# Nine steps of an attention period laid out anew: the seven products in the first five, another order of query and key tiles

## The chip, the cores and the metric

The kernel runs on one core of a Trainium2 chip. The metric is device time in microseconds (us) of one execution. All arithmetic shown is float32, except the small bfloat16 helpers named below.

## The reference, cut to what matters

```python
x = L0_attn_x                                      # (8, 1024, 512)
x = _layernorm(x + attention(x, W_Q, W_K, W_V, W_O))
x = _layernorm(x + moe(x, router_w, router_b, expert_w, expert_b))
# attention: 16 heads of 32, causal
Q, K, V = x @ W_Q.T, x @ W_K.T, x @ W_V.T
probs = softmax(where(causal, Q K^T / sqrt(32), -inf))
y = (probs V) @ W_O.T
# moe: 8 experts, the one with the largest router probability, times that probability
```

The softmax needs the sum of each row, and the kernel also takes each row's extreme first.

## The kernel before

**Periods and steps.** There are B = 8 batches and NG = 4 groups of HG = 4 heads, so NP = 32 periods `n`, each for one batch `b` and one head group `g = n % 4`. A period has NU = 9 steps `u`. One step does, for three different periods at once:

1. the exact scores and their exponentials of period n (`exps`, L806): a bfloat16 matmul that puts in the row constants (L820), four heads' matmuls K·Q on top (L826), two ScalarE exponentials from PSUM to `p` (L832, the first head alone, then the other three), and on the diagonal blocks GpSimd's `affine_select` (L836). `s_units` says which key tile `j` and query half `c` a step takes: one pair, or two pairs that share 512 columns.
2. the row extremes of a later unit, LEAD = 12 units ahead (`maxima`, L697): four heads' matmuls (L709) into four tiles of the pool `ps_m`, then for each head a VectorE pass that writes the raw scores to SBUF and takes the row minimum of the negated scores (L719). `m_units` says which query tile `qt` and which columns a unit takes: query tile 7 first, 3 last. Some units hold two parts, so their VectorE passes are twice as many and half as long. The raw rows live in NRAW = 7 buffers; ScalarE later takes exp with the row's own constant and sums it (`exp_sums`, L744, its instruction L762), as many rows in a step as a credit allows, or as the next unit's need of buffers forces. After the last row of a period ScalarE takes Ln (L750, with two table loads), VectorE splits the result in three bfloat16 parts (`split_maxima`), and `turn_maxima` in the last step transposes them (L783) and copies them to `mT` (L787).
3. a fill of 16 or 32 TensorE instructions: either a product of the queries' and keys' projection two periods ahead, or a whole projection (V, or the output projection, or in batch 0 the router's preparation).
4. the values matmul of the step (`values`, L850, L863) and its addition into `ctx` (copy L882 where it is the first, add L886 otherwise).

**The seven products.** The projection to Q and K of a period is made as a two by two block product with seven instead of eight products (`class seven`). Each product is eight matmul pairs (L629), each of seven is evacuated by VectorE into one or two places of Q and K (L642 add, L646 copy). GpSimd makes their operands, sums of blocks of x and of weights (L606): `begin` (three sums, first and second operand), `second`, `third`, `fourth`, each queued at the end of a step. Before, the products lie in steps 0 (two), 1, 2 (two), 3 and 5; a "short" step is one with one product, `HALVES_AT = (1, 3, 5)`. Whole projections lie in `WHOLE_AT = (4, 6, 7, 8)`. In a short step the fourth head's minimum is put behind the product's evacuation.

**Order.** The program is written out by hand under a manual schedule, each engine's queue in the order of the calls. In a step VectorE has: minima of three or four heads, a `normalize` of finished output rows if the step is "quiet" (L942), the fill's evacuation, the deferred head, small matmuls' evacuation, the `ctx` addition, then statistics of output rows. The PSUM is divided as `ps_m` (four banks in rotation: four heads' maxima, the second product of a step, small matmuls, values), `ps_f` (one bank, shared by the first head's scores and the fill) and `ps_s` (three banks, the other heads' scores). Small matmuls are the router's logits (L990, 8 or 16 instructions as rows of the trace count them) and the turn of logits (L1009). Batch b+1's x is loaded in period g = 1 (`load_x`, SP queue) into the buffers that batch b used. `pieces` are parts of the routing of tokens, which start after period 26 and are put into quiet steps. Before the first period there are LEAD lead steps with maxima and a fill only; after the last period comes the experts' part, one tile after the other.

```python
for u in range(NU):
    t = n * NU + u + LEAD
    exps(n, u)
    ...
    left = maxima_at(t, HG - 1 if short else HG)
```

Of the kernel before, what the change touches and what calls it, by code (L numbers as in the profile page):

```python
# [26 lines left out]
def attn_moe_kernel(ctx: ExitStack, tc: tile.TileContext, x, xT, wqT, wkT, wvT, woT, rwT, rb, ewT, eb, out):  # L27
# [446 lines left out]
    def attention():  # L474
# [10 lines left out]
        with ExitStack() as st:  # L485
# [72 lines left out]
            def run(made, name):  # L558
                out, rest = made(bank(name, ps_f))
                out()  # L560
                if rest:
                    rest()
# [24 lines left out]
            class seven:  # L587
# [45 lines left out]
                def steps(self):  # L633
# [11 lines left out]
                    def copy(dst):  # L645
# [3 lines left out]
                        0: [self.product(self.s, self.t[0], copy(k[1])), self.product(a11, b11, copy(q[0]))],  # L649
                        1: [self.product(self.s, self.t[1], add((q[1], q[0])))],  # L650
                        2: [
                            self.product(a12, b21, add((q[0], q[0]))),
                            self.product(a22, self.t[0], add((q[1], q[1]), op=ALU.subtract)),
                        ],
                        3: [self.product(self.s, b22, add((k[0], k[1])))],
                        5: [self.product(self.s, self.t[1], add((q[1], q[1]), (k[1], k[1])))],
                    }, {0: self.second, 1: self.third, 3: self.fourth}
# [29 lines left out]
            m_units = [[part(7, 0, 512)], [part(7, 512, 1024)]]  # L687
            m_units += [[part(6, 0, 512)], [part(6, 512, 896), part(0, 0, 128, 384, 896)]]
            m_units += [[part(5, 0, 512)], [part(5, 512, 768), part(1, 0, 256, 256, 768)]]
            m_units += [[part(4, 0, 512)], [part(4, 512, 640), part(2, 0, 384, 128, 640)]]  # L690
            m_units += [[part(3, 0, 512)]]
# [42 lines left out]
            HALVES_AT = (1, 3, 5)  # L734
            WHOLE_AT = (4, 6, 7, 8)
# [56 lines left out]
            s_units = [((0, 0),), ((0, 1), (0, 3)), ((0, 2), (1, 6)), ((1, 0),), ((1, 5), (1, 7)), ((1, 1),), ((1, 4),)]  # L792
            s_units += [((1, j),) for j in range(2, 4)]
# [3 lines left out]
            def blocks(u):  # L797

                at = 0
                for c, j in s_units[u]:  # L800
                    q0 = max(c * 512, j * P)
                    w = c * 512 + 512 - q0
                    yield c, j, q0, w, at
                    at += w

            def exps(n, u):  # L806
# [10 lines left out]
                for c, j, q0, w, at in blocks(u):  # L817
# [15 lines left out]
                for c, j, q0, w, at in blocks(u):  # L833
# [16 lines left out]
            def values(n, u, pool=ps_m):  # L850
# [5 lines left out]
                for c, j, q0, w, at in blocks(u):  # L856
# [4 lines left out]
                    for h in range(HG):  # L861
# [4 lines left out]
                            start=new, stop=(c, j) == [x for x in s_units[u] if x[0] == c][-1],  # L866
                        )
                    if g == NG - 1 and c == NC - 1:
                        v_free.append(v_slot.pop((b, j)))
# [156 lines left out]
            LEAD = NU + 3  # L1026
# [26 lines left out]
            for c in range(NC):  # L1053
                for name in ("wq", "wk"):
                    run(project_qk(0, c, name), f"{name}_0_{c}")
# [19 lines left out]
            for n in range(NP):  # L1075
# [21 lines left out]
                late = HALVES_AT[1]  # L1097
                if g == 0:
                    if b:
                        small_ones[late].append(lambda ps: logits_part(b - 1, [NG - 1], False, ps))  # L1100
                    small_ones[HALVES_AT[2]].append(lambda ps: logits_part(b, [0, 1], True, ps))
                elif g == 1:
                    if b:
                        small_ones[HALVES_AT[2]].append(lambda ps: turn_logits(b - 1, ps))
                    small_ones[late].append(lambda ps: logits_part(b, [2, 3], True, ps))
# [7 lines left out]
                for u in range(NU):  # L1113
# [3 lines left out]

                    quiet = u not in behind and (u != HALVES_AT[-1] or n + 3 >= NP)

# [34 lines left out]
                    if g == 1 and b + 1 < B and u == late:  # L1154
                        for c in range(NC):
                            load_x(b + 1, c)
# [74 lines left out]
```

## Time and profile before

| what | value |
|---|---|
| times of three runs | 2178.26, 2180.58, 2180.76 us (median 2180.58) |
| the profiled execution | 2186.84 us, span 2184.9 us |
| granted TensorE clock, mean | 0.993 |
| TensorE matmul busy | 2110.7 us (97%) |
| VectorE, ScalarE, GpSimd busy | 1629.0 (75%), 1547.2 (71%), 784.6 (36%) us |
| before the first scores | 0 to 82.73 us |
| periods 0 to 25 | 82.7 to 1536.9 us |
| the experts' part | about 1880 to 2184.9 us |

Period 11 (head group 3) starts at 692.87 us; the lengths of its nine steps, from first score matmul to first score matmul, are 6.48, 5.18, 6.50, 5.20, 6.81, 5.41, 6.71, 6.50 and 7.17 us, in all 55.96 us. Periods 8, 9, 10 and 11 (head groups 0 to 3) start at 523.75, 580.05, 636.53 and 692.87 us, period 12 at 748.83 us.

Line numbers are those of the kernel before. An instruction group is named by line, engine, operation, and out<-in with the program's tile names. A bracket "[0.59 <-DVE big L642]" says that the engine sat idle so long before the instruction and what ended it. A TensorE row counts an instruction's records, two for one float32 matmul here, and overlaps with its neighbours; its busy time includes time in which a started group waits.

### The profile page before, as it was taken

The page shows a single profiled execution, that of the slowest core. Times are in us where ns is not written, and L with a number is a line of the kernel's source. Part 1 is how long each engine was busy: PE and PEld are TensorE (multiplying, and loading weights), DVE is VectorE, ACT ScalarE, POOL GpSimd, SP SyncE. Part 2 cuts the span into 40 slices and gives each one's busy share as a digit, 9 for nine tenths or more (in the row PEclk, how much of TensorE's full clock was granted, in tenths as well). Part 3 has the DMA queues.
Part 4 walks back from the last instruction along what each step waited for, and adds up shares of the span by engine and source line. Part 5 has one row for each costly group of instructions (what it writes and reads, how often), then busy time and mean ns, then how long its engine had stood idle before and what let it go on. Part 6 is the DMA issues. An engine that isn't in the chain of part 4 may idle for free. (4 is left out here: it accounts for less than half of the span.)

```text
span 2184.9 us, 52442 instructions
## 1 busy us (share of the span) xinstructions
PE 2110.7 (97%) x20251; PEld 829.7 (38%) x20251; DVE 1629.0 (75%) x4960; ACT 1547.2 (71%) x2979; POOL 784.6 (36%) x757
## 2 busy tenths in 40 slices
PE   8989999999999999999999999999999888999998
PEld 2333333333333333333333333333333333344443
DVE  4777777877787778777877787778778885478776
ACT  3688877788777777777777787777777576243443
POOL 3233333333333333333333333333333243255554
PEclk9999999999999999999999999999999999999999
DMA  3001000110021002100210020001001032443432
GB/s 117 1 18 48 1 2 11 69 40 1 7 73 40 2 2 73 45 2 2 74 45 2 2 73 16 31 1 65 20 11 45 7 126 74 135 150 126 135 125 83
DMA packets 46743, 103.79 MB, mean 48 GB/s; under 512 B 5982, under 2 KB 8030, under 8 KB 46368
## 3 DMA queue, kind: packets, MB, share of 16 engines
q1 hardware_dynamic: 34464, 65.02, 8.6%
q0 software_dynamic: 11360, 35.40, 5.1%
q8 instruction: 161, 2.64, 0.5%
q14 instruction: 86, 0.70, 0.1%
q10 hardware_dynamic: 672, 0.02, 0.0%
HBM read 66.87 MB, written 35.39 MB: 47 GB/s over the span
## 5 line engine op out<-in xcount | busy, mean ns | idle before, releaser
L832 ACT ACTIVATE p<-s 128x512 f32<-128x512 f32 x584 | 559.0, 1010 | 396.0 <-PE s L826 395.9
L762 ACT ACTIVATE raw<-raw,low 128x1024 f32<-128x1024 f32 (+7 forms) x1024 | 779.1, 770 | 44.4 <-DVE low L719 44.4
L719 DVE CUSTOM_DVE_ANT_0 raw<-m,wide_mask 128x512 f32<-128x512 f32 (+3 forms) x1024 | 571.5, 587 | 148.9 <-PE m L709 148.9
L836 POOL TENSOR_SCALAR_AFFINE_SELECT p<-p 128x512 f32<-128x512 f32 x256 | 158.8, 639 | 810.5 <-ACT p L832 810.5
L719 DVE CUSTOM_DVE_ANT_0 raw<-m,wide_mask,lowA 128x256 f32<-128x256 f32 (+3 forms) x512 | 273.3, 548 | 140.3 <-PE m L709 140.3
L863 PE MATMUL pv<-p,V 128*32 128x512 f32 (+3 forms) x3072 | 307.6, 493 | 21.0 <-DVE lowA L719 7.1
L709 PE MATMUL m<-big 32*128 32x512 f32 (+3 forms) x3072 | 316.4, 488 | 0.0
L826 PE MATMUL s<-big 32*128 32x512 f32 (+3 forms) x3072 | 313.8, 491 | 0.0
L606 POOL TENSOR_TENSOR xs<-big 128x1024 f32<-128x1024 f32 x60 | 142.4, 2373 | 351.6 <-PE f L629 351.6
L437 PE MATMUL y<-big,gT 128*128 x568 | 255.8, 594 | 2.6 <-ACT gT L429 2.6
L674 PE MATMUL f<-big 128*32 128x512 f32 x2048 | 233.0, 595 | 0.0
L926 PE MATMUL f<-wo,ctx 128*32 128x512 f32 x1920 | 218.4, 595 | 0.8 <-ACT p L832 0.8
L709 PEld LDWEIGHTS m<-big 32*128 32x128 f32 x3072 | 175.2, 186 | 87.7 <-issue 64.3
L762 ACT ACTIVATION_READ_ACCUMULATOR raw<-raw,low 128x1 f32 x1024 | 199.7, 195 | 0.0
L629 PE MATMUL f<-xs,ws 128*32 128x512 f32 x1440 | 173.2, 598 | 1.1 <-ACT p L832 0.9
L886 DVE TENSOR_TENSOR ctx<-pv,ctx 128x384 f32<-128x384 f32 (+2 forms) x250 | 146.7, 587 | 32.8 <-PE pv L863 31.0
L863 PEld LDWEIGHTS pv<-p,V 128*32 128x32 f32 x3072 | 90.6, 110 | 201.4 <-issue 95.1
L820 PE MATMUL s<-mT,ones_b 3*128 3x512 bf16 (+3 forms) x1536 | 132.5, 331 | 23.0 <-DVE big L642 8.9
L826 PEld LDWEIGHTS s<-big 32*128 32x128 f32 x3072 | 142.8, 188 | 21.2 <-issue 15.9
L437 PEld LDWEIGHTS y<-big,gT 128*128 128x128 f32 x568 | 102.6, 191 | 105.7 <-issue 101.7
L455 ACT ACTIVATE yrstd<-ymv,eps 128x1 f32<-128x1 f32 x71 | 20.9, 295 | 151.5 <-DVE ymv L453 146.5
L464 POOL DMA_INDIRECT out<-g,r_sca x71 | 83.2, 1172 | 123.4 <-ACT g L463 90.1
(229 smaller groups left out, 2253.7 us busy)
## 6 DMA issues: line engine op xcount, KB each, us to landing
h<-in_x SPq DMA_DIRECT2D x64, 256.0 KB, 3.8
x<-h SPq DMA_DIRECT2D x64, 256.0 KB, 2.0
big<-in_xT SPq DMA_DIRECT2D x15, 1024.0 KB, 7.3
big<-in_ewT SPq DMA_DIRECT2D x8, 1024.0 KB, 8.0
bias<-in_eb SPq DMA_DIRECT2D x1, 2048.0 KB, 12.0
g<-x,r_gat POOLq DMA_INDIRECT x71, 3.5
out<-g,r_sca POOLq DMA_INDIRECT x71, 2.9
big<-in_xT SPq DMA_DIRECT2D x4, 256.0 KB, 5.7
```

The source lines that it names most:

```text
L437: nc.tensor.matmul(y_ps, lhsT=gT[:, k, :], rhs=big[:, bass.ds(e, 1), k, :].rearrange("p a o -> p (a o)"), start=(k == 0), stop=(k == NK - 1),)
L629: nc.tensor.matmul(ps, lhsT=w[:, k][:, m], rhs=x[:, k, :], start=start, stop=stop)
L674: lambda ps, k, m, start, stop: nc.tensor.matmul(ps, lhsT=xT_sb[b, c][:, k, o : o + P][:, m], rhs=w_sb["wv"][:, k, :], start=start, stop=stop,
L709: nc.tensor.matmul(tiles[h][:, at : at + c1 - c0], lhsT=Q[n][r, qt * P : (qt + 1) * P], rhs=K[n][r, c0:c1], start=True, stop=True,)
L719: nc.vector.tensor_tensor_reduce(out=raws[n, h][:, to : to + w], in0=tiles[h][:, at : at + w], in1=wide_mask[:, 640 - w :] if last else wi ...
L762: nc.scalar.activation(a[:, to : to + w], a[:, to : to + w], AF.Exp, scale=-1.0, bias=low[n][:, qt, h : h + 1], accum_out=sums[n][:, qt, h ...
L826: nc.tensor.matmul(tiles[h][:, at : at + w], lhsT=K[n][r, j * P : (j + 1) * P], rhs=Q[n][r, q0 : q0 + w], start=False, stop=True,)
L832: nc.scalar.activation(p[:, hs], scores, AF.Exp, scale=-1.0)
L836: nc.gpsimd.affine_select(out=p[:, :, at : at + P], in_=p[:, :, at : at + P], compare_op=ALU.is_ge, fill=0.0, base=0, pattern=[[0, HG], [1 ...
L863: nc.tensor.matmul(ps[h * HD : h * HD + HD, parts[c][1] - w : parts[c][1]], lhsT=V[b, j][:, ch : ch + HD], rhs=p[:, h, at : at + w], start ...
L886: nc.vector.tensor_tensor(to, here[:, new:], to, ALU.add)
L926: lambda ps, k, m, start, stop: nc.tensor.matmul(ps, lhsT=ctx_of(b * NG + k, qt * P, P)[:, m], rhs=w_sb["wo"][:, k, :], start=start, stop= ...
```

## The change

It moves work among the nine steps and alters three orders:

- the products: step 0 one, step 1 two, step 2 one, step 3 two, step 4 one; the product with two places of evacuation is the second of step 3. Short steps become 0, 2 and 4, whole projections 5 to 8; `fourth` is queued after step 2, `begin` after step 4.
- `m_units` begins with query tile 4 and ends with 7 (tile 3 just before it); `LEAD` is NU + 4 = 13 instead of 12.
- `s_units` begins with (1,0), (0,0); the last period keeps the old order as `s_last`. Buffers of V are freed at a key tile's last use (`last_use`).
- small matmuls go to steps 5 and 6 (in group 1 also to step 1) instead of 3 and 5; quiet steps become 4 to 8 (5 to 8 in group 1); the two halves of the next x are loaded after steps 3 and 4.
- the first four projections use the four banks of `ps_m` in place of the one of `ps_f`.

```diff
-            def run(made, name):
-                out, rest = made(bank(name, ps_f))
+            def run(made, name, pool=ps_f):
+                out, rest = made(bank(name, pool))
...
-                        0: [self.product(self.s, self.t[0], copy(k[1])), self.product(a11, b11, copy(q[0]))],
-                        1: [self.product(self.s, self.t[1], add((q[1], q[0])))],
-                        2: [
-                            self.product(a12, b21, add((q[0], q[0]))),
+                        0: [self.product(self.s, self.t[0], copy(k[1]))],
+                        1: [self.product(a11, b11, copy(q[0])), self.product(self.s, self.t[1], add((q[1], q[0])))],
+                        2: [self.product(self.s, b22, add((k[0], k[1])))],
+                        3: [
                             self.product(a22, self.t[0], add((q[1], q[1]), op=ALU.subtract)),
+                            self.product(self.s, self.t[1], add((q[1], q[1]), (k[1], k[1]))),
                         ],
-                        3: [self.product(self.s, b22, add((k[0], k[1])))],
-                        5: [self.product(self.s, self.t[1], add((q[1], q[1]), (k[1], k[1])))],
-                    }, {0: self.second, 1: self.third, 3: self.fourth}
+                        4: [self.product(a12, b21, add((q[0], q[0])))],
+                    }, {0: self.second, 1: self.third, 2: self.fourth}
...
-            m_units = [[part(7, 0, 512)], [part(7, 512, 1024)]]
+            m_units = [[part(4, 0, 512)], [part(4, 512, 640), part(2, 0, 384, 128, 640)]]
+            m_units += [[part(5, 0, 512)], [part(5, 512, 768), part(1, 0, 256, 256, 768)]]
             m_units += [[part(6, 0, 512)], [part(6, 512, 896), part(0, 0, 128, 384, 896)]]
-            m_units += [[part(5, 0, 512)], [part(5, 512, 768), part(1, 0, 256, 256, 768)]]
-            m_units += [[part(4, 0, 512)], [part(4, 512, 640), part(2, 0, 384, 128, 640)]]
-            m_units += [[part(3, 0, 512)]]
+            m_units += [[part(3, 0, 512)], [part(7, 0, 512)], [part(7, 512, 1024)]]
...
-            HALVES_AT = (1, 3, 5)
-            WHOLE_AT = (4, 6, 7, 8)
+            HALVES_AT = (0, 2, 4)
+            WHOLE_AT = (5, 6, 7, 8)
...
-            s_units = [((0, 0),), ((0, 1), (0, 3)), ((0, 2), (1, 6)), ((1, 0),), ((1, 5), (1, 7)), ((1, 1),), ((1, 4),)]
-            s_units += [((1, j),) for j in range(2, 4)]
+            s_units = [((1, 0),), ((0, 0),), ((1, 1),), ((0, 2), (1, 6)), ((1, 2),), ((1, 5), (1, 7)), ((1, 4),)]
+            s_units += [((0, 1), (0, 3)), ((1, 3),)]
+
+            s_last = [s_units[i] for i in (1, 7, 3, 0, 5, 2, 6, 4, 8)]
+            last_use = {j: u for u, unit in enumerate(s_units) for _, j in unit}
...
-                    if g == NG - 1 and c == NC - 1:
+                    if g == NG - 1 and last_use[j] == u:
                         v_free.append(v_slot.pop((b, j)))
...
-            LEAD = NU + 3
+            LEAD = NU + 4
...
-                    run(project_qk(0, c, name), f"{name}_0_{c}")
+                    run(project_qk(0, c, name), f"{name}_0_{c}", ps_m)
...
-                late = HALVES_AT[1]
+                late = WHOLE_AT[0]
                 if g == 0:
+                    small_ones[late].append(lambda ps: logits_part(b, [0, 1], True, ps))
                     if b:
-                        small_ones[late].append(lambda ps: logits_part(b - 1, [NG - 1], False, ps))
-                    small_ones[HALVES_AT[2]].append(lambda ps: logits_part(b, [0, 1], True, ps))
+                        small_ones[late + 1].append(lambda ps: logits_part(b - 1, [NG - 1], False, ps))
                 elif g == 1:
+                    small_ones[1].append(lambda ps: logits_part(b, [2, 3], True, ps))
                     if b:
-                        small_ones[HALVES_AT[2]].append(lambda ps: turn_logits(b - 1, ps))
-                    small_ones[late].append(lambda ps: logits_part(b, [2, 3], True, ps))
+                        small_ones[late].append(lambda ps: turn_logits(b - 1, ps))
...
-                    quiet = u not in behind and (u != HALVES_AT[-1] or n + 3 >= NP)
+                    quiet = u not in behind and (n + 3 >= NP or u not in ((3, 4) if g == 1 else (3,)))
...
-                    if g == 1 and b + 1 < B and u == late:
-                        for c in range(NC):
-                            load_x(b + 1, c)
+                    if g == 1 and b + 1 < B and u in (3, 4):
+                        load_x(b + 1, 4 - u)
```

## The prediction

> Times in a step count from its first score matmul (L820); s, m, f, pv are the TensorE parts scores (L820/L826), maxima (L709), fill, values (L863). A period n is nine steps u.
>
> **What bounds it now.** First the page: TensorE leads.
>
> ```profile
> span 2184.9 us, 52442 instructions
> ...
> PE 2110.7 (97%) x20251; PEld 829.7 (38%) x20251; DVE 1629.0 (75%) x4960; ACT 1547.2 (71%) x2979; POOL 784.6 (36%) x757
> ```
>
> Then the table of windows, cut at the steps of period 11: its length is 55.96 us, and the neighbours of the same head group differ by 0.01. So one period, counted well, is the kernel. Columns: window, length, busy time and count of each engine.
>
> ```profile
> 711.03:716.23 5.20, 5.20 (x56) 1.83 (x52) 3.74 (x11) 4.35 (x10) 1.04 (x1) 1.00 0.00 0
> 716.23:723.04 6.81, 6.81 (x92) 2.94 (x89) 4.96 (x22) 5.37 (x12) 2.56 (x3) 1.00 0.02 4
> 723.04:728.45 5.41, 4.83 (x48) 1.58 (x44) 3.73 (x10) 4.27 (x11) 1.26 (x1) 1.00 0.00 0
> 728.45:735.16 6.71, 6.70 (x60) 2.23 (x61) 4.38 (x12) 4.60 (x10) 3.15 (x4) 1.00 0.01 2
> sum 55.96, PE 55.28 PEld 20.84 DVE 40.25 ACT 44.63 POOL 18.39; mean PE 6.14 PEld 2.32 DVE 4.47 ACT 4.96 POOL 2.04
> ```
>
> TensorE idles 0.68 us of a period, yet more is lost. The timeline of TensorE, then of VectorE, over the short step u=5 and the start of u=6 (start, us, engine, line, operation):
>
> ```profile
> 725.09 1.92 PE L629 MATMUL f<-xs,ws 128*32 128x512 f32 x16
> 726.83 1.04 PE L863 MATMUL pv<-p,V 128*32 128x512 f32 x8
> 728.46 0.40 PE L820 MATMUL s<-mT,ones_b 3*128 3x512 bf16 x4 [0.59 <-DVE big L642]
> 729.54 1.24 PE L709 MATMUL m<-big 32*128 32x512 f32 x8
> ```
> ```profile
> 727.12 1.28 DVE L642 TENSOR_TENSOR big<-big,f 128x512 f32<-128x512 f32 x2
> 728.32 0.68 DVE L719 CUSTOM_DVE_ANT_0 raw<-m,wide_mask 128x512 f32<-128x512 f32 x1
> 728.92 0.69 DVE L886 TENSOR_TENSOR ctx<-pv,ctx 128x512 f32<-128x512 f32 x1
> ```
>
> Three rules follow. (a) Scores share the one bank of `ps_f` with the fill before: they start 0.06 after its outputs (728.40 to 728.46). (b) With four banks in `ps_m`, the fourth head of m takes the bank of the pv before: m ends 1.17 after that ctx add (729.61 to 730.78), so 1.24 stands for 1.04 where the add ends more than about 0.94 into the step; in two-part maxima it is 1.25 (u=4: add to 717.41, m to 718.66). (c) The fill needs ScalarE's first exp of the step. Where that is late, it starts 0.63 after the exp does, and 0.07 before m's end otherwise:
>
> ```profile
> 1568.48 1.04 PE L709 MATMUL m<-big 32*128 32x512 f32 x8
> 1570.23 1.07 PE L629 MATMUL f<-xs,ws 128*32 128x512 f32 x8 [0.71 <-ACT p L832]
> ```
> ```profile
> 1569.60 1.92 ACT L832 ACTIVATE p<-s 128x512 f32<-128x512 f32 x2
> ```
>
> ScalarE's pace, from its timeline in u=0 of period 11: a 896+128 row costs 1.41 (696.04 to 697.45), and rows start 1.82 after the exps (694.22).
>
> ```profile
> 694.22 1.94 ACT L832 ACTIVATE p<-s 128x512 f32<-128x512 f32 x2 [1.86 <-PE s L826]
> 696.04 1.04 ACT L762 ACTIVATE raw<-raw,low 128x896 f32<-128x896 f32 x1
> 697.07 0.40 ACT L762 ACTIVATE raw<-raw,low 128x128 f32<-128x128 f32 x1
> 697.45 1.04 ACT L762 ACTIVATE raw<-raw,low 128x896 f32<-128x896 f32 x1
> ```
>
> The Trainium skill ("Perfetto Trace Analysis", Identifying the Most-Contended Engine) says that matmul busy share is no good measure of headroom. By busy share 0.68 us could be won here; by the rules above, u=1 (0.3, POOL's select), u=4 (0.23), u=5 (0.6) and u=6 (0.2) lose 1.3. I go by the latter.
>
> **The change, step by step.** Matmuls, minima, row sums and selects are the same in number; only 31 VectorE ops go (one a period: first use of a ctx half is now a whole copy). So this is about where waits fall. Bare lengths from the table: two products 6.48 (u=0); one product 4.77 (u=5: f at 2.05, pv ends 4.83, next scores 0.06 before); whole fill with two-block scores 6.56 (f at 2.11, rest 4.45 as in u=4); whole fill 6.48; with turned maxima 7.17 (u=8).
>
> - u=0, one product. VectorE: three heads from 2.24 at 0.61 end at 4.07, output 0.68 to 4.75; scores of u=1 start at 4.81 by (a). The fourth head and the ctx copy then end at 5.97, 1.16 into u=1.
> - u=1, two products, two-part maxima: m ends 1.16+1.25=2.41, f at 2.34 for 2.05: 6.48+0.29=6.77.
> - u=2, one product: 4.81 like u=0. But ScalarE's order here is two rows of 896+128 and one of 512 (0.70 as in u=6), because row tile 3 is one step long and the next step needs four fresh buffers: 1.33+1.82+2×1.41+0.70=6.67, that is 1.86 into u=3.
> - u=3, two products: the first exp at 1.86, not 1.36, so f at 2.49 for 2.06 by (c): 6.50+0.43=6.93. This hides the 0.2 that (b) would take there. Now the two-place product comes last: f ends 6.13, two adds to 7.48, two ctx adds to 8.13, 1.20 into u=4.
> - u=4, one product: m ends 1.20+1.18, f at 2.31: 4.77+0.26=5.03. Its output (after f, 4.29 to 4.97) just hides. Last head and ctx add end 1.22 into u=5.
> - u=5, whole fill, two-block scores: m ends near 2.43, f at 2.36, 2.36+4.45=6.81.
> - u=6, 7, 8: 6.48, 6.56, 7.17; nothing late (ScalarE with its two table loads ends 1.2 into u=7, needed at 1.4).
>
> Sum 55.37. The small matmuls (router logits) leave steps where a wait hid part of them, for long steps where nothing does: 16 cost 0.86, 8 cost 0.44 (u=3: 5.64 against 5.20), the turn of four 0.67 (as u=8 over u=7). Head group 0 gets 16+8, group 1 16 and a turn, group 2 16 plus 0.32 for a normalize (L942) that now falls in short u=4, group 3 eight: 56.67, 56.90, 56.55, 55.81. Before, from the starts of successive periods: 56.29, 56.48, 56.34, 55.96. Differences +0.38, +0.42, +0.21, -0.15: mean +0.215, over 24 steady periods **+5.2**.
>
> POOL: the products' sums (xs 2.4, ws 0.74, big 1.28) still end before use: third's xs starts at u=1's f end (5.98), ends 1.7 into u=2, needed at 2.05; fourth's at 1.6 into u=3, used by the second product at 4.3. `begin` after u=4 runs in the select-free stretch. In group 1 it waits for `load_x`, now split over SP at u=3 and 4: at 7.3 us (page, median landing) xs starts 4.9 into u=4 and the ws end 3.7 into u=5, selects run 0.2 late, pv is not due until 5.8: nothing. Behind that load SP holds only h loads and stores that nothing in u=4 reads. If the landing took 3 us more, pv would wait about 1.5, seven times: +10.
>
> **Ends.** Start: four projections on four banks lose the three 0.81 waits (2.4), but m's fourth head then waits for the last copy: gain 1.7. Lead: one more maxima step without fill; VectorE's four two-part heads (3.0) go ahead of the router mean and the copy of the maxima, which the first scores wait for: +3.0. Net +1.3. Periods 0 and 1, whose fills are short: ScalarE's 6.3 in u=6 overruns a step of 5.06: +0.7. Tail (periods 26 to 31, with the routing's pieces on VectorE, now after u=4 to 8): one step's minima gone (2.45 of VectorE, of which GpSimd's four 0.67 fills of a step, L289, cover a part), the Ln a step earlier, but the 6 us slot piece now delays short u=4. Bounds -7 (both in full, and the 2.0 that period 26 takes over its kin now) and +5 (that piece in full); I take -2, nearest to the row of minima.
>
> The clock there: after an idle gap of 3.3 us at 1741.1 a pv took 1.94 for 1.04 and the windows show 0.97 granted. The skill ("TensorE: Matmul & The Clock Gate", The HAM clock gate) puts the half clock after about 3.4 us idle; the new gap in that period would be nearly 4 us, so it changes nothing, while without the gate the tail would gain some 1.5.
>
> Total: 5.2+0.7+1.3-2=**+5.2 us**. The profiled execution took 2186.84 (span 2184.9); it would become 2192. Against the median 2180.58, 6 lower, that is **2185.8**. Changes within 0.2% (4.4 us) can hardly be told from none.
>
> **Rivals.**
> 1. Faster: the bank waits (b) do not follow from short steps as I lay them (0.29 in u=1, 0.26 in u=4, 0.25 in u=5). For it: in u=2 of the old layout VectorE ends long steps early enough. Against: u=6 shows the same sequence. Without them 24×0.8=19 less: 2166.6. Decided by whether the ctx add ends before 0.94. Chance 0.2.
> 2. Slower: ScalarE's chain, not only u=2: if the rows after the table loads in u=6 run over the 0.2 left, u=7 waits 0.3 to 0.5 in every period; with that 24×0.45=11: 2196.6. For it, ScalarE works 44.6 of 56 us. Chance 0.15.
> 3. No change: exposed small matmuls and new waits exactly eat the removed ones and the tail gains 6 instead of 2: 2181. Chance 0.2.
>
> **Numbers.** My layout has 0.45: its steady term is good to 0.25 a period (6 us) and the tail to 5, so about 0.27 of it is over +4.4, 0.13 within, 0.05 below. Slower 0.27+0.15+0.03=0.45, same 0.13+0.15=0.28, faster 0.05+0.2+0.02=0.27. The range 2167 to 2197 reaches from the first rival to the second; its own case alone is 2178 to 2194.
>
> **What would show it.** Right: u=3 about 6.93 with f waiting for p; m of u=1, 4, 5 longer than 1.04; scores after one-product steps without the 0.6 idle; period 55.8 in group 3, near 56.7 in 0 to 2; first scores near 84. Wrong: exp of u=3 at 1.4, m everywhere 1.04, or a wait on DMA or a select in u=5.

## The result, and the profile after

The changed kernel takes 2194.05 us (median of 4 runs, 2193.81 to 2194.45) against 2180.67 for the kernel before beside it (4 runs, 2178.26 to 2183.37): ratio 1.0062, 95% interval 1.0048 to 1.0076. It is slower, by 13.4 us. The forecast was 2185.8 in a range of 2167 to 2197: the range holds the time, the sign is the one that had most chance, and the size is short by 8.2 us. The layout's own case had been put at 2178 to 2194, so the time lies at its upper edge; the wider range comes from the rivals. Executions of one program differ here by several us, because TensorE's clock falls to half for short stretches that are not the same each time; the accounts below therefore go by traces, stage by stage.

The page of the profile after. Line numbers of the changed kernel are a few higher: maxima L710, minima L720, row sums L763, scores L824 and L830, exponentials L836, values L867, `ctx` L886 (copy) and L890 (add), copy of the maxima L788.

```profile
span 2192.2 us, 52340 instructions
...
PE 2125.6 (97%) x20251; PEld 855.3 (39%) x20251; DVE 1633.7 (75%) x4929; ACT 1544.1 (70%) x2979; POOL 785.4 (36%) x757
```

TensorE has the same 20251 instructions and 14.9 us more busy time: waits inside started groups and half clock count as busy. VectorE has the 31 instructions fewer that were foretold. Then the windows of period 11, cut at its first score matmuls (window, length, busy time and count of TensorE, weight loads, VectorE, ScalarE and GpSimd, then the granted clock and the DMA):

```profile
698.79:703.62 4.83, 4.83 (x49) 1.72 (x45) 3.27 (x9) 3.33 (x6) 0.75 (x1) 1.00 0.86 276
703.62:710.32 6.70, 6.70 (x69) 2.83 (x70) 5.53 (x21) 5.37 (x11) 3.54 (x4) 1.00 0.00 1
710.32:715.20 4.88, 4.87 (x49) 1.87 (x46) 3.32 (x9) 4.32 (x11) 4.39 (x4) 1.00 0.01 3
715.20:722.08 6.88, 6.77 (x80) 2.83 (x81) 5.01 (x14) 5.84 (x14) 3.50 (x4) 1.00 0.00 0
722.08:727.21 5.13, 5.13 (x49) 1.79 (x46) 4.07 (x11) 3.06 (x4) 3.17 (x3) 1.00 0.01 3
727.21:734.40 7.19, 7.19 (x92) 2.96 (x89) 4.77 (x13) 5.32 (x8) 1.22 (x2) 1.00 0.00 0
734.40:740.91 6.51, 6.51 (x73) 2.32 (x70) 4.33 (x18) 5.11 (x7) 0.63 (x1) 1.00 0.02 5
740.91:747.48 6.57, 6.57 (x85) 2.52 (x82) 5.14 (x16) 6.42 (x15) 1.22 (x2) 1.00 0.01 2
747.48:754.65 7.17, 7.17 (x81) 2.86 (x78) 4.93 (x19) 5.72 (x14) 0.00 (x0) 1.00 0.00 0
sum 55.86, PE 55.73 PEld 21.70 DVE 40.39 ACT 44.51 POOL 18.43; mean PE 6.19 PEld 2.41 DVE 4.49 ACT 4.95 POOL 2.05
```

TensorE now idles only 0.13 us of this period, where it idled 0.68, and the period is 0.10 shorter. That is group 3. In groups 0, 1 and 2 the periods are 56.70, 56.99 and 56.52, that is 0.41, 0.51 and 0.18 longer than before.

All accounts cut the span at the same places: the first scores, the first scores of periods 2 and 26, and those of the last step (u=8 of period 31). Two traces of each kernel, the second ones from the runs "again" and "after2" below:

| us | before | before, second | after | after, second |
|---|---|---|---|---|
| ahead of the first scores | 82.73 | 82.91 | 83.55 | 84.62 |
| periods 0 and 1 | 103.62 | 103.40 | 106.59 | 107.03 |
| 24 steady periods | 1350.50 | 1350.51 | 1356.58 | 1356.58 |
| periods 26 to 31 | 335.76 | 329.19 | 333.17 | 329.73 |
| rest, the experts' part | 312.31 | 312.31 | 312.30 | 313.40 |
| span | 2184.9 | 2178.3 | 2192.2 | 2191.4 |

The steady periods repeat to 0.01 us. Against the second trace of before, the two traces of after show +13.9 and +13.0, of which 6.1 is steady in both; the other 7 to 8 lie at the ends of the span, and not at the same place in both.

### The profile page after: what moved, and what is told of

It reads as the page before. It is cut to its first block, busy times and chain, and to the rows that moved or that the text cites. A ratio compares the mean times of both kernels' runs of the same rounds, so it can differ in the third digit from the quotient of the medians.

```text
span 2192.2 us, 52340 instructions
## 1 busy us (share of the span) xinstructions
PE 2125.6 (97%) x20251; PEld 855.3 (39%) x20251; DVE 1633.7 (75%) x4929; ACT 1544.1 (70%) x2979; POOL 785.4 (36%) x757
## 3 DMA queue, kind: packets, MB, share of 16 engines
q8 instruction: 161, 2.64, 0.5%
## 5 line engine op out<-in xcount | busy, mean ns | idle before, releaser
L836 ACT ACTIVATE p<-s 128x512 f32<-128x512 f32 x584 | 558.2, 1009 | 401.9 <-PE s L830 397.2
L763 ACT ACTIVATE raw<-raw,low 128x640 f32<-128x640 f32 (+7 forms) x1024 | 779.7, 769 | 47.6 <-DVE low L720 47.6
L720 DVE CUSTOM_DVE_ANT_0 raw<-m,wide_mask 128x512 f32<-128x512 f32 (+3 forms) x1024 | 569.3, 587 | 146.3 <-PE m L710 145.7
L720 DVE CUSTOM_DVE_ANT_0 raw<-m,wide_mask,lowA 128x384 f32<-128x384 f32 (+3 forms) x512 | 275.5, 548 | 120.0 <-PE m L710 119.8
L710 PE MATMUL m<-big 32*128 32x512 f32 (+3 forms) x3072 | 333.6, 491 | 0.0
L867 PE MATMUL pv<-p,V 128*32 128x512 f32 (+3 forms) x3072 | 305.9, 491 | 17.8 <-DVE lowA L720 5.7
L830 PE MATMUL s<-big 32*128 32x512 f32 (+3 forms) x3072 | 316.4, 494 | 0.0
L710 PEld LDWEIGHTS m<-big 32*128 32x128 f32 x3072 | 190.6, 186 | 89.8 <-issue 71.3
L763 ACT ACTIVATION_READ_ACCUMULATOR raw<-raw,low 128x1 f32 x1024 | 199.9, 195 | 0.0
L890 DVE TENSOR_TENSOR ctx<-pv,ctx 128x512 f32<-128x512 f32 (+2 forms) x250 | 144.2, 587 | 39.8 <-PE pv L867 39.8
L867 PEld LDWEIGHTS pv<-p,V 128*32 128x32 f32 x3072 | 95.5, 110 | 186.3 <-issue 134.7
L606 POOL TENSOR_TENSOR xs<-xs,big 128x1024 f32<-128x1024 f32 x30 | 71.0, 2366 | 262.2 <-PE f L629 262.2
L824 PE MATMUL s<-mT,ones_b 3*128 3x512 bf16 (+3 forms) x1536 | 133.8, 330 | 20.2 <-DVE mT L788 9.2
L830 PEld LDWEIGHTS s<-big 32*128 32x128 f32 x3072 | 143.8, 188 | 20.9 <-issue 15.4
L642 DVE TENSOR_TENSOR big<-big,f 128x512 f32<-128x512 f32 x180 | 120.8, 685 | 29.1 <-PE f L629 22.5
```

Source lines behind the costliest of these rows:

```text
L606: nc.gpsimd.tensor_tensor(out, a, b, op)
L710: nc.tensor.matmul(tiles[h][:, at : at + c1 - c0], lhsT=Q[n][r, qt * P : (qt + 1) * P], rhs=K[n][r, c0:c1], start=True, stop=True,)
L720: nc.vector.tensor_tensor_reduce(out=raws[n, h][:, to : to + w], in0=tiles[h][:, at : at + w], in1=wide_mask[:, 640 - w :] if last else wi ...
L763: nc.scalar.activation(a[:, to : to + w], a[:, to : to + w], AF.Exp, scale=-1.0, bias=low[n][:, qt, h : h + 1], accum_out=sums[n][:, qt, h ...
L830: nc.tensor.matmul(tiles[h][:, at : at + w], lhsT=K[n][r, j * P : (j + 1) * P], rhs=Q[n][r, q0 : q0 + w], start=False, stop=True,)
L836: nc.scalar.activation(p[:, hs], scores, AF.Exp, scale=-1.0)
```

## The experiments

**Is the profiled time of before typical?** The kernel before, unchanged, traced and timed again.

> The kernel before, once more, for a second trace. Its profiled execution took 2186.84 us and its other runs 2178 to 2183, while those of the changed kernel agree within 0.7 us. Theory: the steady periods repeat to 0.01 us (56.29, 56.48, 56.34, 55.96), and the 6 us come from single places, in the tail of the attention part (from 1536.9 us) or in the experts' part. Then this trace has the same start (first scores at 82.7) and the same period starts up to number 26, and a shorter rest. Rival: the spread lies in the periods; then their lengths differ by 0.2 each.

Measured: 2180.43 us median (10 runs, 2179.72 to 2186.98), ratio 1.0003 (0.9988 to 1.0018). The new trace has the same steady periods, and a tail of 329.19 us where the first had 335.76. So the execution that the forecast started from, 2186.84, was one of the longer ones, and all of its excess lay in the tail. The difference is the clock. An early spot shows it most cleanly: windows of the first trace of before, then of the second, over the same work of period 0 (same columns as above).

```profile
108.00:112.00 4.00, 2.06 (x29) 1.21 (x32) 4.00 (x18) 4.00 (x10) 1.22 (x2) 1.00 0.00 0
112.00:115.40 3.40, 3.40 (x24) 0.96 (x20) 0.07 (x1) 2.24 (x4) 0.00 (x0) 0.50 0.02 5
```
```profile
108.00:112.00 4.00, 2.06 (x28) 1.04 (x28) 3.91 (x18) 4.00 (x10) 1.22 (x2) 1.00 0.00 0
112.00:115.40 3.40, 3.40 (x36) 1.23 (x36) 1.57 (x6) 2.98 (x5) 0.00 (x0) 1.00 0.02 5
```

In both TensorE is busy 2.06 of the first 4 us (idle gaps of 1.12 and 0.82). In one the clock is 0.50 in the next 3.40 us and 24 records fit; in the other it is 1.00 and 36 fit. The second execution pays at 122.8 instead. In the tail the first has 6.8, 10.2 and 6.8 us at half clock (from 1740.2, 1777.7 and 1832.3), the second 3.4 and 3.4.

**Do rules (a) and (b) hold?** The fourth head of the maxima is no longer put behind the evacuation in short steps.

```diff
-                    short = u in HALVES_AT and n + 2 < NP
+                    short = False
```

> The changed kernel without the rule that defers the fourth head of the maxima (and the ctx add behind it) in the three short steps: all four heads go to VectorE ahead of the fill's output. Theory (rules a and b of the prediction: scores start 0.06 after the fill's output; the long step's m is slow because the ctx add falls into it): the fourth head moves 0.6 ahead of the output, so the steps u=0, 2, 4 take 5.43, 5.45, 5.6 for 4.83, 4.88, 5.13, and u=1 gives back 0.2 to 6.48 and u=3 up to 0.4, 6.5 to 6.9; net +0.8 a period, about +20 us in the steady periods, the whole near 2214. Rival (what fixes the short steps is TensorE or ScalarE, and the head's place is free): short steps stay within 0.1, the whole within 4 us of the changed kernel's 2194.

Measured (one run): 2218.21 us, steady periods 1377.08, which is 20.5 more. Windows of u=0 to 3 of period 11:

```profile
706.18:711.62 5.44, 4.83 (x49) 1.74 (x46) 3.88 (x11) 3.34 (x6) 1.36 (x1) 1.00 0.78 246
711.62:718.10 6.48, 6.48 (x68) 2.46 (x68) 4.78 (x19) 5.16 (x11) 2.94 (x4) 1.00 0.00 0
718.10:723.54 5.44, 4.87 (x49) 1.88 (x46) 4.01 (x12) 5.10 (x11) 4.97 (x4) 1.00 0.01 3
723.54:730.04 6.50, 6.50 (x80) 2.64 (x81) 4.41 (x12) 5.39 (x14) 2.95 (x4) 1.00 0.00 0
```

And TensorE's timeline around the end of u=0, where the next scores now wait (the bracket gives idle time and releaser):

```profile
709.96 1.04 PE L867 MATMUL pv<-p,V 128*32 128x512 f32 x8
711.62 0.40 PE L824 MATMUL s<-mT,ones_b 3*128 3x512 bf16 x4 [0.61 <-DVE big L646]
```

One head's minimum, 0.61 us, moved ahead of the copy to `big`, and the step is 0.61 longer with the same TensorE busy time: rule (a). The long step u=1 falls to the bare 6.48 at the same time, because the `ctx` copy behind the head moved too: rule (b). In u=3, which falls to the bare 6.50, two things move: its maxima take 1.04 again, rule (b), and ScalarE's exponential starts 1.35 into the step instead of 1.81, since u=2 before it is 0.56 longer, rule (c). The step times are those that the theory gave, to 0.05 us where it named one. Deferring the head pays: it costs 0.22, 0.38 and 0.21 in u=1, 3 and 5 and wins 0.61, 0.56 and 0.44 in u=0, 2 and 4.

**Is u=3 late by ScalarE's rows (rule c)?** Step 0 no longer has a reduced budget of row sums, so that fewer rows are left for u=2.

```diff
-            per_step = (HG * sum(row_cost(qt) for qt in range(NQT)) + LOG + SHORT * len(HALVES_AT)) / NU
+            per_step = (HG * sum(row_cost(qt) for qt in range(NQT)) + LOG + SHORT * len(HALVES_AT[1:])) / NU
...
-credit[0] = min(credit[0], 700) + per_step - (SHORT if (t - LEAD) % NU in HALVES_AT else 0)
+credit[0] = min(credit[0], 700) + per_step - (SHORT if (t - LEAD) % NU in HALVES_AT[1:] else 0)
```

> The changed kernel with step 0 no longer given a smaller share of ScalarE's row sums, so that one row fewer is left to step 2. Theory: ScalarE ends 0.85 into step 3, its exp starts at 1.36 there, and the bank wait comes out behind it: f at 2.26 instead of 2.45, step 3 at 6.70 instead of 6.89; step 1 is no worse, since its late exp (1.65) falls within the bank wait. 0.19 times 30: 5 us less, 2189. If the bank wait is not there, step 3 goes to 6.50 and 11 us are won; if ScalarE was not what held step 3, nothing moves.

Measured: steady 1352.78, 3.8 less than the changed kernel; u=3 takes 6.70 for 6.88, u=1 6.74 for 6.70; time 2190.64 (4 runs, 2187.65 to 2194.80), ratio to before 1.0059 (1.0042 to 1.0076). The exponential of u=3 in the changed kernel (ScalarE), then the maxima and the fill of the same step (TensorE):

```profile
716.31 0.71 ACT L763 ACTIVATE raw<-raw,low 128x512 f32<-128x512 f32 x1
...
717.01 1.91 ACT L836 ACTIVATE p<-s 128x512 f32<-128x512 f32 x2
```
```profile
716.29 1.24 PE L710 MATMUL m<-big 32*128 32x512 f32 x8
717.64 1.92 PE L629 MATMUL f<-big,ws 128*32 128x512 f32 x16
```

The exp starts 1.81 into the step, right behind a row, and the fill 0.63 after it, at 2.44. With the row moved (ScalarE, TensorE; this u=3 starts at 713.57):

```profile
714.92 1.94 ACT L836 ACTIVATE p<-s 128x512 f32<-128x512 f32 x2 [0.46 <-PE s L830]
```
```profile
714.67 1.24 PE L710 MATMUL m<-big 32*128 32x512 f32 x8
715.84 1.92 PE L629 MATMUL f<-big,ws 128*32 128x512 f32 x16
```

The exp is on time and waits for its scores. The fill now follows the maxima, whose 1.24 still carries the bank wait: 6.70, not the bare 6.50. So (c) hid the 0.2 of (b), as the forecast had it.

**Is u=4 late by the `ctx` add?** The two products of u=3 change places, so that the one with two places of evacuation comes first.

```diff
-                            self.product(a22, self.t[0], add((q[1], q[1]), op=ALU.subtract)),
                             self.product(self.s, self.t[1], add((q[1], q[1]), (k[1], k[1]))),
+                            self.product(a22, self.t[0], add((q[1], q[1]), op=ALU.subtract)),
```

> The changed kernel with the two products of step 3 in the other order, so that the one with two places comes first. Theory (a late ctx addition holds the next maxima's fourth bank): the two adds lie under the second product, the ctx adds end 0.9 into step 4 instead of 1.25, its maxima end at 2.11 instead of 2.46, and step 4 takes 4.9 instead of 5.12: 0.23 times 30, some 7 us less, near 2187. Step 3 stays at 6.89 and step 5 as it is. Rival (short steps are limited by VectorE's whole load): step 4 stays at 5.12, 2194.

Measured: u=4 takes 4.90 (5.36 in group 2) for 5.13, u=3 takes 6.98 for 6.88; steady 1354.36, 2.2 less; time 2189.50 (4 runs), ratio 1.0049 (1.0032 to 1.0065). With the product of one place last, m of u=4 is back at 1.03 (it ran from 1.08 to 2.11 into the step, where it had run to 2.46), so rule (b) set that step too. The expectation was 0.23 a period, 5.5 us in the 24, with u=3 unchanged; less than half of it came. In group 2 u=4 gains nothing, and in u=3 the fill starts 2.54 instead of 2.44 into the step. ScalarE is not the reason there: its exponential starts 1.81 into u=3 in both kernels, and the fill follows 0.73 after it instead of 0.63. The first product now reads other operands, sums made by GpSimd, but these had ended at 1.68 into the step; the 0.1 stays open.

**What do the small matmuls cost?** The router's logits and their turn go to the short steps u=2 and u=4, where the TensorE work is shortest.

```diff
-    small_ones[late].append(lambda ps: logits_part(b, [0, 1], True, ps))
+    small_ones[2].append(lambda ps: logits_part(b, [0, 1], True, ps))
...
-    small_ones[1].append(lambda ps: logits_part(b, [2, 3], True, ps))
+    small_ones[2].append(lambda ps: logits_part(b, [2, 3], True, ps))
...
-    small_ones[late].append(lambda ps: turn_logits(b - 1, ps))
+    small_ones[4].append(lambda ps: turn_logits(b - 1, ps))
```

> The changed kernel with its small matmuls moved back into short steps: the 16 or 8 logit matmuls to step 2 in every group, in group 0 the eight of the batch before to step 4, in group 1 the turn to step 4. Theory (step 3 waits for ScalarE because step 2 is short; small matmuls are only paid in full where no wait is behind them): step 2 grows to 5.7 (5.3 in group 3) and step 3 falls from 6.89 to 6.50 (6.55); step 5 of group 1 loses 0.2 of bank wait too. Groups 0 to 3 at 56.2, 56.4, 56.1 and 55.5 instead of 56.70, 56.99, 56.52 and 55.86; 12 us less, near 2182. Rival (the price of a small matmul is the same everywhere): periods unchanged, 2194.

Measured: steady 1344.97, 11.6 less than the changed kernel and 5.5 less than before. Time 2178.26 (10 runs, 2176.20 to 2180.35), ratio 0.9995 (0.9986 to 1.0005): no difference from before. Windows of u=2, 3 and 5 in period 11, which has 8 logits:

```profile
707.31:712.54 5.23, 5.23 (x56) 2.10 (x52) 3.67 (x9) 4.67 (x11) 4.76 (x4) 1.00 0.02 3
712.54:719.22 6.68, 6.68 (x84) 2.77 (x81) 5.00 (x15) 5.50 (x14) 3.16 (x4) 1.00 0.01 2
...
724.35:731.13 6.78, 6.78 (x85) 2.73 (x82) 4.44 (x12) 5.32 (x8) 1.22 (x2) 1.00 0.00 0
```

u=5 loses 0.41. u=2 gains 0.35, and u=3 loses 0.20: the longer u=2 gives ScalarE the time that it lacked. With 16 logits (groups 0 to 2) u=2 takes 5.66, 0.78 more, u=3 falls to the bare 6.50, and u=5 to between 6.56 and 6.78 from 7.46 to 7.63. So the matmuls cost nearly as much in the short steps as in the long ones; what is won is mostly the 0.20 to 0.39 that u=3 gives back. So the two parts of the change can be told apart: the tiles and products laid out anew are worth 5.5 us in the steady periods, and putting the small matmuls into long steps takes back 11.6. That the total stays at the kernel before's comes from the start: 108.20 for periods 0 and 1, with half clock from 81.2, 125.6 and 183.6.

**The start.** Three kernels, one run each. First, the four first projections back on one bank:

```diff
-                    run(project_qk(0, c, name), f"{name}_0_{c}", ps_m)
+                    run(project_qk(0, c, name), f"{name}_0_{c}")
```

> The changed kernel with the first four projections of the lead back on the one bank of the fills, as before the change. Theory (prediction: four banks lose three waits of 0.81 and make m's fourth head wait for the last copy, net gain 1.7): first scores 1.7 later than in the changed kernel, 85.2; all behind them the same, whole +1.7. Rival (VectorE's chain, not TensorE, sets the time of the first scores): first scores within 0.5 of 83.55.

Measured: first scores at 85.94. The runs that share the lead of the changed kernel have them between 83.10 (swap) and 84.71 (best2, below), so the four banks are worth 1.2 to 2.8; the theory's 1.7 lies inside, the rival's 0.5 does not. Most of that spread is the arrival of the first inputs. Counted from the end of the first projection, the first scores come 72.3 us later in all nine traces that share this lead up to the last maxima step, 74.5 later here and 71.4 later in the kernel before: the banks are worth 2.2, and the whole lead costs 0.9. The whole run took 2201.56, 7.5 more than the changed kernel where the theory had 1.7 more; its trace has 13.7 us of half clock in periods 0 and 1 against 10.2, and 20.5 in the tail.

Second, the router mean and the turn of the first maxima ahead of the last maxima step:

```diff
+                if t == LEAD - 1:
+                    center_router()
+                    turn_maxima(0, bank("mT_ps_0"))()
...
-                if t == LEAD - 1:
-                    center_router()
-            turn_maxima(0, bank("mT_ps_0"))()
```

> The changed kernel with the router mean and the turn of the first maxima put ahead of the last maxima step of the lead, not behind it. In the changed kernel TensorE idles 0.92 and 1.78 us there and the first scores start at 83.55; the clock is at half from 81.5 to 88.4 and the first step takes 7.10 us for 4.83. Theory (the idle time ahead of the first scores comes from VectorE's last four two-part heads, and the half clock from that idle time): first scores about 3 us earlier, 80.5, no half clock there, first step near 4.9, so the first two periods near 104 us for 106.59 and the whole 4 to 6 us shorter than the changed kernel. Rival (the half clock has another cause, or the heads only move behind the first scores): first scores 80.5 to 82, but the half clock stays within the first step and the first step grows by what was won; whole within 2 us of the changed kernel. Steady periods 56.7, 57.0, 56.5, 55.9 in both.

Third, eight matmuls without use in the gap ahead of the first scores:

```diff
             turn_maxima(0, bank("mT_ps_0"))()
+            warm = bank("warm", ps_f)
+            for i in range(8):
+                nc.tensor.matmul(warm, lhsT=ident_b, rhs=parts[:, 4 * (i % 2) : 4 * (i % 2) + 4].rearrange("p q h d -> p (q h d)"), start=True, stop=True)
```

> The changed kernel with eight extra matmuls of 512 columns (about 0.24 us each, their output is never read) behind the turn of the first maxima, where TensorE otherwise idles 1.78 us ahead of the first scores. Theory (the half clock from 81.5 to 88.4 comes from that idle time, and from it the first step's 7.1 us): first scores within 0.3 of 83.55, clock 1 there, first step 4.8 to 5.0, the first two periods 104.3 for 106.59. Rival (the 0.92 of idle time ahead of the router mean is enough, or the half clock comes from something other than idle time): a half clock of at least 3.4 us still within 81 to 89 and a first step over 6. Steady periods and tail as in the changed kernel (tail 329 to 335).

Windows at the first scores, of the changed kernel and then of the one with the eight matmuls:

```profile
81.52:84.90 3.38, 1.59 (x16) 0.92 (x17) 1.89 (x12) 1.18 (x4) 0.00 (x0) 0.50 0.00 0
84.90:88.36 3.46, 3.46 (x20) 0.81 (x16) 0.67 (x3) 2.48 (x3) 0.00 (x0) 0.50 0.00 0
```
```profile
81.52:84.90 3.38, 3.22 (x29) 2.01 (x33) 2.76 (x16) 2.05 (x8) 0.00 (x0) 1.00 0.00 0
84.90:88.36 3.46, 3.46 (x36) 1.06 (x32) 1.69 (x5) 2.65 (x4) 0.00 (x0) 1.00 0.00 0
```

With the gap filled the clock stays at 1.00 and the first step takes 4.83 for 7.10; the theory for this step holds. Of all traces, the seven with the unfilled gap and this lead all show half clock over the first step, for 3.4 or 6.8 us, and the two with the eight matmuls ("warm" and "best3") show none. The whole gained less: the first scores came at 84.43, and periods 0 and 1 took 106.01 for 106.59, since the clock was at half for 3.4 us from 123.9 and from 181.9, in steps with short fills. The second kernel shows the rival: first scores at 81.83, but the second ones at 90.67 (changed kernel: 90.65; the first projection ended 0.8 later in this run, so 0.8 of the 2.5 is kept). TensorE's timeline there:

```profile
82.93 3.37 PE L710 MATMUL m<-big 32*128 32x512 f32 x8
86.23 3.61 PE L629 MATMUL f<-xs,ws 128*32 128x512 f32 x16
...
90.67 0.40 PE L824 MATMUL s<-mT,ones_b 3*128 3x512 bf16 x4
```

The maxima take 3.37, because VectorE's heads now stand behind the first scores and hold the banks; then the fill takes 3.61 for 1.92, at half clock from 86.3. The times, 2192.51 and 2191.52, lie within the scatter of the changed kernel, 2190.80 to 2194.45.

**A version that beats both.** The edits of "small", "swap" and "lead", and no `normalize` in u=4 of groups 0, 2 and 3 (`quiet` false there); "best2" is the same without the edit of "lead", "best3" is best2 with the eight matmuls.

```diff
-    quiet = u not in behind and (n + 3 >= NP or u not in ((3, 4) if g == 1 else (3,)))
+    quiet = u not in behind and (n + 3 >= NP or u not in (3, 4))
```

> The changed kernel with four edits together: the router logits in the short steps u=2 and 4 (alone: steady periods 11.6 us shorter over 24, but the first two periods 1.6 longer), the ctx add of the last head before the fourth part's subtraction in u=3 (alone: u=4 4.90 for 5.13, u=3 0.09 longer), no normalize in u=4 of group 2, and the router mean and turn of the lead ahead of its last maxima step. Theory (terms add): steady 1342 us for 1356.6, first scores near 80.5, first two periods 104 to 106, tail 330; whole 2168 to 2174, faster than before by 0.3 to 0.6%. Rival (the clock at the start and in the tail takes back what is won, as in the run with the logits alone): whole 2176 to 2181, the same as before.

> The four edits that beat both kernels without the one in the lead (router mean and turn of the first maxima back behind the last maxima step). Theory (that edit only moves VectorE's heads behind the first scores, where the first step pays for them: alone its second scores started at 90.67 against 90.65): steady periods 1338.5 as with all four, second scores near 90.4, whole 2171 to 2176, not to be told from the 2173.1 of all four. Rival (it won the 3 us that its first scores came earlier): 2176 to 2179.

> The three edits (router logits in short steps, ctx add ahead in u=3, no normalize in u=4) with the eight extra matmuls ahead of the first scores. Theory (the half clock at the start comes from the idle time and costs the first step 2.2): first step 4.8 to 5.0, second scores near 88.3, whole 2 us under the same without these matmuls, 2169 to 2174. Rival: first step still over 6, whole the same as without them.

Measured: 2173.13 us (7 runs, 2171.33 to 2174.91), ratio to before 0.9963 (0.9950 to 0.9977); best2 2174.13, ratio 0.9968 (0.9956 to 0.9980); best3 2174.08, ratio 0.9965 (0.9951 to 0.9978). All three are faster than both kernels and not to be told apart, so neither edit at the start shows in the whole. In "best2" the first two periods have 6.8 us of half clock at the first scores; in "best3", with the gap filled, the same 6.8 us fall as 3.4 at 123.5 and 3.4 at 181.5. Steady periods take 1338.46, 1338.40 and 1338.27: 12.1 less than before, 18.1 less than the changed kernel. Of these 12, a part is lost at the ends again: against the second trace of before, "best" takes 3.5 more in periods 0 and 1 and 3.3 more in the tail, where one step (u=7 of period 26) waits 2.12 for an exponential and then runs at half clock; its tail holds 23.9 us of half clock, that trace of before 6.8.

**Is the tail's loss the program's?** The changed kernel, unchanged, again.

> The changed kernel unchanged, traced and timed again. Theory (steady layout +6.1 and a start of +3.8 belong to the program; the tail's +4.0 is the half clock's draw, since runs with the same tail program show 329.5, 329.9, 333.2 and 334.1): steady periods 1356.5 again, tail anywhere from 329 to 335, times spread over at least 4 us, from 2189 to 2196, ratio to before 1.004 to 1.007. Rival (the tail's loss belongs to this layout): tail 333 again, all times within 1 us of 2194.

Measured: 2193.72 us (6 runs, 2190.80 to 2194.16), ratio 1.0056 (1.0041 to 1.0071); steady 1356.58 again, tail 329.73. So the tail of 333.17 does not belong to the program: the same code gave 329.73. The spread, 3.4 us, is a little under the 4 of the theory, and five of six runs lie within 1.2 us; in the two traces, though, the sum is made up differently. Four more runs with the same code in the tail show 334.09 (psf), 329.46 (lead), 329.86 (warm) and, with changed steady steps, 330.96 (swap).

The windows' granted clock tells these tails apart. With the same tail code, 10.2 us at half clock go with 329.46, 329.73 and 329.86, and 20.5 us with 333.17 and 334.09; in the kernel before 6.8 us go with 329.19 and 23.9 with 335.76. In both kernels a microsecond of half clock adds 0.39 to the tail. By these lines, an estimate, the changed tail is 0.8 us shorter than the old one at the same amount of half clock.

## Why the prediction was right or wrong

**The steady layout: right, step by step.** The forecast had 4.81, 6.77, 4.81, 6.93, 5.03 for u=0 to 4, and the trace shows 4.83, 6.70, 4.88, 6.88, 5.13. Periods of groups 0 to 3 were put at 56.67, 56.90, 56.55 and 55.81, and are 56.70, 56.99, 56.52 and 55.86. The signs asked for are all there: the late exp in u=3 (above), no idle time ahead of scores after a step with one product, and longer maxima in u=1, 4 and 5. TensorE's timeline at u=1, at u=4 and at u=5:

```profile
703.62 0.40 PE L824 MATMUL s<-mT,ones_b 3*128 3x512 bf16 x4
703.83 1.04 PE L830 MATMUL s<-big 32*128 32x512 f32 x8
704.69 1.26 PE L710 MATMUL m<-big 32*128 32x384 f32 x16
...
723.17 1.37 PE L710 MATMUL m<-big 32*128 32x512 f32 x8
...
728.35 1.25 PE L710 MATMUL m<-big 32*128 32x512 f32 x8
```

The largest step error is u=4 (+0.10): m, held up by two `ctx` adds, ended 2.46 into the step where 2.38 was put. In sum the steady periods came out at +6.1 for +5.2.

**The small matmuls: right.** Where nothing hides them, 16 cost 0.86 (u=1 of group 1: 7.56 for 6.70), 8 cost 0.41 (u=6 of group 0: 6.92 for 6.51). The forecast took the places of these matmuls as given; "small" shows that other places are worth 11.6 us, more than the 6.1 of the steady change.

**The ends: mis-sized, and this is where most of the 8.2 us are.** Forecast, then the two traces of after less the second of before:

| term | forecast | after | after, second |
|---|---|---|---|
| lead | +1.3 | +0.6 | +1.7 |
| periods 0 and 1 | +0.7 | +3.2 | +3.6 |
| steady | +5.2 | +6.1 | +6.1 |
| tail | -2 | +4.0 | +0.5 |
| experts' part | 0 | 0.0 | +1.1 |
| sum | +5.2 | +13.9 | +13.0 |

Lead: the four banks gained 2.2 for the 1.7 put, and the rest of the lead cost 3.1 for the 3.0, so +0.9 for +1.3; what the table shows beside that is the arrival of the first inputs.

Periods 0 and 1: the steps with short fills did grow, in u=6, 7 and 8 (5.36, 6.01, 5.96 for 5.06, 5.57, 5.39), where the forecast looked at u=6 alone. Without the half clock these periods would be longer by about 0.65 (period 0: warm 52.28 less 1.06 for u=7, against 52.21 less 1.64 in the second trace of before) and 0.90 (period 1: 52.09 in "lead" against 51.19), together 1.55 for the forecast's 0.7. The rest is the clock: the new wait ahead of the first scores put 6.8 us of half clock over the first step, 2.27 us (2.64 in the second trace), which the kernel before does not have. The forecast saw that wait and priced it as time alone.

Tail: the step that failed is "so it changes nothing", said of the clock there, and the -2 taken for the layout. Of the layout: u=8 of period 28 did become 1.2 shorter (11.17 to 9.96) and u=3 of period 29 3.8, but u=7 of period 29 became 4.35 longer (4.67 to 9.02); at the same amount of half clock the tail is about 0.8 shorter by the estimate above, where 2 was put. Its +4.0 and +0.5 go with the half clock, 20.5 and 10.2 us of it against 6.8 in the trace compared with.

The clock of the whole, from the timed executions, says the same. All ten of the changed kernel had a mean granted clock of 0.992 to 0.994; of 64 of the kernel before, 51 had 0.995 to 0.998 and 13 had 0.992 to 0.994. At 0.993 the kernel before took 2186.0 to 2187.2 us (11 executions) and the changed one 2193.0 to 2194.2 (6), medians 7.4 apart, and the terms without the clock (steady 6.1, short fills 1.55, lead 0.9, tail -0.8) add up to 7.7. So about 6 of the 13.4 us, an estimate, are half clock that the kernel before mostly does not have, and for which the forecast had nothing. Of these the new wait ahead of the first scores brings 2.3 and 2.6 in the two traces of the changed kernel; which waits bring the rest was not traced. The other errors are small: 0.9 in the steady periods, 0.85 in the short fills, 1.2 in the tail, -0.4 in the lead.

**The profiled execution.** Its span plus the sum of terms would have been 2190.1; the trace of after has 2192.2. That looks like an error of 2 us, and is not: the trace of before happened to hold 23.9 us of half clock in its tail where its second trace held 6.8, and this cost it 6.6 us. The median was the right base, and the comparison of one profile with one profile would have hidden the error of the ends.

**The rivals.** Rival 1 (no bank waits) fell: m takes 1.24 to 1.37 in four steps, and "shortoff" takes those of u=1, 3 and 5 away, "swap" that of u=4. Rival 2 gave 2196.6, nearer to the result than the forecast, by a mechanism that did not occur: u=7 takes 6.57, 0.01 over the forecast, with ScalarE at 6.42 of it. Rival 3 (the parts cancel) fell for the kernel as changed. The ratio of "small", 0.9995, is what it had named, but there a steady gain is eaten by the start, not by small matmuls. POOL and the split load of x caused nothing in the steady steps: pv of u=5 follows the fill and the logits there.

## What to carry to other kernels

Cut two traces at the same work, stage by stage, before explaining a difference in total: here the steady part repeats to 0.01 us and the ends differ by 6 us between executions of one program, with the half clock. Comparing executions of the same granted clock separates the two. Small matmuls on a full TensorE were not free in any step here, but put ahead of a step that starts late for another engine they buy that engine time: 8 and 16 of them cost 0.35 and 0.78 in u=2, and u=3 gave back 0.20 and 0.39. A new wait on TensorE ahead of a burst is to be priced twice, once as the wait and once as the burst at half clock: the one ahead of the first scores made the step behind it 2.3 and 2.6 us longer in the two traces of the changed kernel.

## What the runs showed of the hardware

TensorE's half clock does not need long idle time here: it began at 112.0 us in one execution of before after gaps of 1.12 and 0.82 us, and did not begin after the same gaps in another. The stretches measured are 3.4, 6.8 and 10.2 us, multiples of 3.4, and in each of the 14 traces they start on one grid: in the first trace of before at 112.0, 1740.2, 1777.7 and 1832.3 us, that is 477, 11 and 16 steps of 3.413 apart. The Trainium skill ("TensorE: Matmul & The Clock Gate", The HAM clock gate) tells of an activity window of about 3.4 us that runs freely, and the lengths and the differences between executions agree with that; its table asks for an idle window of about that length, and here the longest gap in front of the stretch at 112.0 was 1.12 us, so the measurement decides. What share of a window has to be idle was not measured.

In the kernel "lead" the clock fell at 86.3 us although TensorE shows as busy from 82.93 on: its maxima took 3.37 us, because their matmuls came one head at a time, 0.75 apart, as VectorE freed the banks. So a row that is busy in the profile does not mean that the clock holds. Nor does it have to fall: in "best" the same group took 3.37 us (from 81.68), the clock stayed at 1.00, and the fill behind it took 1.92. What decides between the two was not measured.
